# Macaron block on one core: contraction tiles of every eighth channel, both second-pass tiles of a pair transposed from blocks by way of DRAM, third layernorm's statistics on ScalarE

## The chip, the core and the metric

The kernel runs on one core of a Trainium2 chip. The metric is the device time of one execution in microseconds (us). Before the change three runs gave a median of 1308.92 us (1308.46 to 1311.21).

## What is computed

The input x has 4096 tokens of 1024 channels, all in float32. Three blocks follow each other, each on a layernorm of the running x:

```python
x = x + 0.5 * ffn(layernorm(x), weight, bias, centroids, assignments)
x = x + attn(layernorm(x), Wq, bq, Wk, bk, Wv, bv)
x = x + 0.5 * ffn(layernorm(x), weight, bias, centroids, assignments)

def ffn(x):                                  # weight 1024 x 1024, 64 centroids
    hits = softmax(x @ centroids.T / 0.1) > 0.01
    dense = x @ weight.T + bias
    return where(any(hits, 1)[:, None] & any(hits, 0)[assignments][None, :], dense, 0)

def attn(x):                                 # 32 heads of 32, 8 kv heads
    q, k, v = x @ Wq + bq, x @ Wk + bk, x @ Wv + bv
    scores = einsum('bsdh,bseh->bsde', q, repeat(k)) / sqrt(32)
    return einsum('bsde,bseh->bsdh', softmax(scores), repeat(v))
```

Attention mixes the 32 positions d of the heads within one token, not tokens. Whether a column of the FFN counts depends on all tokens (any over axis 0), so an FFN's mask is known only when every token has been seen.

## The kernel before, in words

There are NT = 32 tiles of 128 tokens. All matrix products run on TensorE, which needs the contracted channels on the partitions, so each normalised tile xn (tokens on partitions, 1024 channels in a row) has to be transposed to xT: eight groups of 128 channels, k = 0 to 7, each 128 channels by 128 tokens. Group k holds the channels 128 k to 128 k + 127, and the weights wc (FFN weight and centroids) and wqkv (the attention's three weights; the four query heads of a kv head are summed ahead) are laid out in the same groups.

There are three passes over the tokens. The first computes the first FFN before masking and writes it to DRAM (d1), the centroid gates, and the masks at its end. The second adds the masked d1 to x, does the attention, and the gate and a part of the third block's FFN. The third finishes the last FFN and stores. Most large products are in Strassen's form as Winograd wrote it: a pair of tiles is taken together, GpSimd forms four sums of their transposed halves (`token_sums`, L242 to L262), and seven smaller products take the place of eight.

The order of instructions is written out by hand: each engine's queue runs in the order in which the code issues, and DMAs are issued from the queues of SyncE (`nc.sync`), GpSimd and ScalarE, also in order. A DMA that reads what an earlier one wrote to DRAM waits on its queue until that one has landed, and what is queued behind waits too.

There are two ways to transpose. `transposed` (L198 to L207) issues eight 128x128 transposes on TensorE into two banks of PSUM, and ScalarE copies each bank out (L206); the banks are taken in turn out of four that the products use as well (`bank`, L155). In the first pass, from tile 5 on, `load_blocks` (L497) loads x in 32x32 blocks, by four DMAs whose runs are 32 channels (128 bytes), one for each strip of 32 partitions, `blocks_normed` (L511) normalises them on ScalarE and `from_blocks` (L518) transposes within the blocks on VectorE. Which block lies where makes the result a transposed tile. The statistics for them come from a second load of x.

The second pass is the loop at L1011 over stages s = 0 to 36. At stage s the tiles s to s+3 are prepared, tile b = s-2 is in the attention, g = s-3 gets its attention result added and its third layernorm, and f = s-4 and a = s-5 are transposed for the third block and gated. Stages 4 to 31 (`PAIRED`) go in pairs, even and odd. The steps of a stage that matter here, in code order:

- `load_2(s+4)`: SyncE loads x and d (d1 of that tile).
- `scores` for tile b (L1019), exponential on ScalarE (L1021).
- `project_two` (L806) gives q, k, v of the pair's tiles by seven products prod(1), (5), (6), (2), (3), (7), (4), advanced step by step by `next(two)`. Each tile's result is stored to DRAM on SyncE (qkvd, L837).
- `transposed` of xn2[s+1] (L1027), if not done yet: the second layernorm's tile.
- `keys` on GpSimd (L881), `second_added` (L967, tile g: ot times rs, then x + ot), the store of x to y2, the use of the gates.
- `sums_normed` (L183): mean and variance of tile s+2 by ScalarE, two passes over the tile with an accumulator, then a square root; its reciprocal on VectorE and the normalisation on ScalarE follow at L1069.
- `weighted` (L917): the softmax weights transposed and summed on VectorE.
- `first_added` (L473): VectorE masks d, GpSimd adds it to x, for tile s+3.
- `gate_2`, `transposed` of xn3[f] (L1074 in odd stages, L1123 in even ones), `attend` (L937) with its store to od on SyncE.
- `moments` (L158) of tile g on VectorE by BATCH_NORM_STATS, then `normed` on ScalarE: the third layernorm (L1090, L1096).
- `rearranged` (L865): SyncE loads qk (one DMA) and v (four) from qkvd; `returned`: SyncE loads ot from od.
- At the end of an odd stage the second tile of the next pair is transposed on TensorE (L1125) and GpSimd forms the pair's `token_sums` (L1126), which prod(5), prod(6), prod(3) and prod(7) of the next pair need.

Of the kernel before, what the change touches and what calls it, by code (L numbers as in the profile page):

```python
# [42 lines left out]
def kernel(  # L43
# [110 lines left out]

    def bank(name):  # L155
        return psum.tile([P, 512], F32, tag="mm", bufs=4, name=name)
# [26 lines left out]
    def sums_normed(src, name):  # L183
# [11 lines left out]
        nc.scalar.activation(xn, src, AF.Identity, bias=sc[:, 1:2], scale=sc[:, 0:1])  # L195
        yield xn

    def transposed(xn, name):  # L198

        t_ = row(f"xT_{name}").rearrange("p (k c) -> p k c", c=P)  # L200
        for h in range(2):
            tp = bank(f"tp_{name}_{h}").rearrange("p (j c) -> p j c", j=4)
            for j in range(4):
                k = 4 * h + j
                nc.tensor.transpose(tp[:, j, :], xn[:, k * P : (k + 1) * P], ident)  # L205
            nc.scalar.copy(t_[:, 4 * h : 4 * h + 4, :], tp)  # L206
        return t_  # L207
# [274 lines left out]
    with (  # L482
# [4 lines left out]
        xb = {}  # L487
# [8 lines left out]

        def load_blocks(t):  # L497

            xb[t] = row(f"xb_{t}").rearrange("p (k i c) -> p k i c", k=KT, i=4)
            src = rows(xf, t).rearrange("(i t) (k j c) -> j t k i c", i=4, j=4, k=KT)  # L500
            for j in range(4):
                nc.sync.dma_start(out=xb[t][strip(j)], in_=src[j])
# [8 lines left out]
        def blocks_normed(t, sb):  # L511
            for i in range(4):
                bi = xb[t][:, :, i]
# [3 lines left out]

        def from_blocks(t):  # L518

            b = xb.pop(t)  # L520
            t_ = row(f"xT_1_{t}")
            nc.vector.transpose(t_, b.rearrange("p k i c -> p (k i c)"))
            return t_.rearrange("p (k c) -> p k c", c=P)
# [8 lines left out]

        cn = row("cn")[:, :512]
        for h in range(2):
            nc.sync.dma_start(
                out=cn[h * NCL : (h + 1) * NCL, :], in_=cent[:, h * 512 : (h + 1) * 512]
            )
# [30 lines left out]
        def columns(c, second=nc.scalar.copy):  # L568

            for h in range(2):  # L570
                tp = bank(f"tpw{c}_{h}").rearrange("p (j c) -> p j c", j=4)
                for j in range(4):
                    k = 4 * h + j
                    nc.tensor.transpose(tp[:, j, :], wn[c][:, k * P : (k + 1) * P], ident)  # L574
# [6 lines left out]
        tp = bank("tpc").rearrange("p (j h c) -> p h j c", j=4, h=2)  # L581
        for j in range(4):
            nc.tensor.transpose(tp[:, :, j, :], cn[:, j * P : (j + 1) * P], ident)
        for h in range(2):
            nc.vector.tensor_copy(wc[:, 4 * h : 4 * h + 4, EMB:], tp[:, h])
# [6 lines left out]
        def weights(t):  # L592


            if 3 <= t < 6 or 11 <= t < 16:
# [4 lines left out]
                    out=qn, in_=wq[k * P : (k + 1) * P].rearrange("p d (g r) -> p (d g) r", r=REP)  # L600
# [8 lines left out]
            elif 16 <= t < 20:  # L609
                k = 2 * (t - 16)  # L610
                kvs = row(f"kv{k}").rearrange("p (k w c) -> p k w c", k=2, w=2)
                for i, src in ((0, wk), (1, wv)):
                    nc.sync.dma_start(
                        out=kvs[:, :, i],
# [172 lines left out]
    with (  # L787
# [223 lines left out]
        for s in range(NT + 5):  # L1011
# [4 lines left out]
            if s == NT + 1:  # L1016
                next(steps)
# [268 lines left out]
```

## Time and profile before

| | |
|---|---|
| median of 3 runs | 1308.92 us |
| the profiled execution | 1309.77 us, of which the span of its instructions is 1308.0 |
| TensorE matmul busy | 1296.1 us, 99% |
| VectorE busy | 876.9 us, 67% |
| ScalarE busy | 490.9 us, 38% |
| GpSimd busy | 602.4 us, 46% |
| granted TensorE clock | 0.997 |
| DMA | 213.44 MB, 163 GB/s; 227624 of 283475 packets under 512 B |
| a pair of stages in the second pass | 34.9 to 35.0 us |

"Busy" is the union of an engine's instructions; matmuls overlap, so a busy TensorE says only that it never ran dry. The chain is the profile's own reconstruction, back from the last instruction: at each step what released it, or what stood ahead of it on its engine. In the names of groups, `tp` is a transpose into PSUM, `qs` a product of project_two, `ff` a product of an FFN part with the centroids, `sc` and `po` the products of the attention, `ts_2q` the token sums of the second pass. PE, DVE, ACT, POOL and SPq are TensorE, VectorE, ScalarE, GpSimd and SyncE's queue. Matmuls in float32 are recorded as two instructions each, transposes as one.

### The profile page before, as it was taken

What the parts mean: (1) busy time and instruction counts of PE and PEld (TensorE: products, weight loads), DVE (VectorE), ACT (ScalarE), POOL (GpSimd) and SP (SyncE); (2) the same over time, 40 slices, a digit from 0 to 9 for tenths busy, and PEclk for the clock granted to TensorE, in tenths of its full rate; (3) what the DMA queues carried; (4) which work ended last, traced back from release to release, by engine and by line L of the source; (5) the groups of instructions that cost most, each with busy time, mean ns of one, the idle gap of its engine ahead of it and who ended that gap; (6) DMA issues with size and microseconds to landing.
All of it is one profiled execution on the core that took longest, in us unless ns stands there. A gap on an engine that the chain in (4) does not pass through costs nothing.

```text
span 1308.0 us, 22703 instructions
## 1 busy us (share of the span) xinstructions
PE 1296.1 (99%) x8734; PEld 841.4 (64%) x8734; DVE 876.9 (67%) x1798; ACT 490.9 (38%) x818; POOL 602.4 (46%) x460
## 2 busy tenths in 40 slices
PE   8999999999999999999999999999999999999998
PEld 7665777777776656666666666666666555555555
DVE  4565557555546367888888888888877448555556
ACT  4433222332211446666666666666632300000000
POOL 2622212412113247566767666666557326633440
PEclk9999999999999999999999999999999999999999
DMA  8866866776214156566666666666452347665522
GB/s 282 161 167 129 187 159 148 171 202 122 65 57 193 57 170 188 144 186 188 192 190 199 201 186 198 182 191 196 124 156 64 105 145 240 225 208 172 177 111 88
DMA packets 283475, 213.44 MB, mean 163 GB/s; under 512 B 227624, under 2 KB 242344, under 8 KB 283368
## 3 DMA queue, kind: packets, MB, share of 16 engines
q1 hardware_dynamic: 265740, 164.51, 46.2%
q0 software_dynamic: 8736, 30.68, 6.4%
q10 hardware_dynamic: 8892, 16.81, 3.6%
q8 instruction: 69, 1.13, 0.4%
q14 instruction: 38, 0.31, 0.1%
HBM read 127.77 MB, written 84.18 MB: 162 GB/s over the span
## 4 chain that ended last, share of the span: by engine, by line
PE 97%; DVE 2%; ACT 0%; DMA 0%; issue 0%; SPq 0%; ACTq 0%
PE st L286 43%; PE qs L825 20%; PE ff L212 14%; PE la L360 6%; PE tp L205 5%; PE pq L212 3%; PE sc L901 2%; PE po L943 2%; PE tpw L574 1%; DMA wn<-in_L_ffn_weight_dram 0%; PE pm L458 0%; DVE d L277 0%; DVE bn L162 0%; DVE best L426 0%; PE warm L544 0%
## 5 line engine op out<-in xcount | busy, mean ns | idle before, releaser
L251 POOL TENSOR_TENSOR ts<-xT 128x512 f32<-128x512 f32 x32 | 42.0, 1314 | 361.7 <-DVE sc L171 166.9
L277 DVE TENSOR_TENSOR d<-st,d 128x384 f32<-128x384 f32 (+1 forms) x162 | 88.8, 550 | 167.9 <-PE st L286 166.6
L212 PE MATMUL ff<-wc,xT 128*128 128x320 f32 x704 | 197.1, 433 | 1.4 <-ACT xT L206 0.6
L286 PE MATMUL st<-wc,xT 128*128 128x384 f32 x512 | 175.8, 486 | 0.0
L212 PEld LDWEIGHTS ff<-wc,xT 128*128 128x128 f32 x704 | 131.9, 190 | 56.4 <-ACT xT L206 1.9
L286 PEld LDWEIGHTS st<-wc,xT 128*128 128x128 f32 x512 | 95.9, 190 | 61.8 <-issue 0.6
L286 PE MATMUL st<-wqkv,ts 128*128 128x384 f32 (+1 forms) x392 | 131.3, 485 | 1.9 <-DVE d L277 1.9
L286 PE MATMUL st<-ws,ts 128*128 128x384 f32 x384 | 131.1, 486 | 0.0
L881 POOL TENSOR_TENSOR kd<-qk,tmask 128x1024 f32<-128x1024 f32 x32 | 60.6, 1895 | 146.2 <-DMA qk<-qkvd 146.2
L825 PE MATMUL qs<-wc,ts_2q 128*128 128x384 f32 x336 | 114.4, 490 | 0.0
L286 PEld LDWEIGHTS st<-wqkv,ts 128*128 128x128 f32 x392 | 74.7, 192 | 53.3 <-POOL x L972 2.5
L464 DVE SCALAR_TENSOR_TENSOR d<-d,qsel,mask 128x1024 f32<-128x1024 f32 (+2 forms) x68 | 106.3, 1564 | 0.2
L475 POOL TENSOR_TENSOR x<-x,d 128x1024 f32<-128x1024 f32 x32 | 75.4, 2357 | 62.7 <-DVE d L464 33.3
L277 DVE TENSOR_TENSOR d<-st,brow 128x384 f32<-128x384 f32 x96 | 52.9, 551 | 75.3 <-PE st L286 75.3
L286 PEld LDWEIGHTS st<-ws,ts 128*128 128x128 f32 x384 | 71.2, 190 | 43.0 <-issue 0.8
L165 ACT ACTIVATE mv<-mv,eps 128x1 f32<-128x1 f32 x66 | 19.4, 295 | 204.6 <-DVE mv L164 204.5
L825 PEld LDWEIGHTS qs<-wc,ts_2q 128*128 128x128 f32 x336 | 62.7, 190 | 43.6 <-issue 2.8
L206 ACT COPY xT<-tp 128x512 f32<-128x512 f32 x138 | 73.2, 582 | 44.6 <-PE tp L205 44.6
L286 PE MATMUL st<-wc,ts 128*128 128x384 f32 x256 | 87.9, 486 | 0.0
L162 DVE BATCH_NORM_STATS2 bn<-x 128x6 f32<-128x512 f32 x132 | 84.2, 680 | 3.3 <-DMA x<-in_L_attn_x_dram 3.3
L825 PE MATMUL qs<-wqkv,xT 128*128 128x384 f32 x224 | 78.3, 492 | 0.0
L972 POOL TENSOR_TENSOR x<-x,ot 128x1024 f32<-128x1024 f32 x32 | 76.3, 2384 | 2.5
(146 smaller groups left out, 2249.4 us busy)
## 6 DMA issues: line engine op xcount, KB each, us to landing
x<-in_L_attn_x_dram SPq DMA_DIRECT2D x64, 512.0 KB
d<-d SPq DMA_DIRECT2D x64, 512.0 KB
out_dram<-x ACTq DMA_DIRECT2D x30, 512.0 KB
xb<-in_L_attn_x_dram SPq DMA_DIRECT2D x108, 128.0 KB
y<-x POOLq DMA_DIRECT2D x26, 512.0 KB, 3.1
xTd<-xT POOLq DMA_DIRECT2D x26, 512.0 KB, 5.6
xT<-xTd SPq DMA_DIRECT2D x26, 512.0 KB
x<-y SPq DMA_DIRECT2D x26, 512.0 KB
```

The lines of the kernel that those rows point to most:

```text
L162: nc.vector.bn_stats(st[:, i, :], src[:, i * 512 : (i + 1) * 512])
L205: nc.tensor.transpose(tp[:, j, :], xn[:, k * P : (k + 1) * P], ident)
L206: nc.scalar.copy(t_[:, 4 * h : 4 * h + 4, :], tp)
L212: nc.tensor.matmul(p, src[:, k, :], wts[:, k, lo:hi], start=(k == 0), stop=(k == KT - 1))
L277: nc.vector.tensor_tensor(out, ps, other, ALU.add)
L286: nc.tensor.matmul(ps, src[:, k, :], wts[:, k, :], start=(k == 0 and onto is None), stop=(k == 3), skip_group_check=onto is not None,)
L360: nc.tensor.matmul(ps, src[:, k, :], wts[:, k, :], start=(k == 0 and onto is None), stop=(k == 3), skip_group_check=onto is not None,)
L464: nc.vector.scalar_tensor_tensor(d[:, sl], d[:, sl], qsel[which][:, t : t + 1], mask[:, sl], ALU.mult, ALU.mult)
L475: nc.gpsimd.tensor_tensor(xt[t], xt[t], dt_.pop(t), ALU.add)
L825: nc.tensor.matmul(ps, src[:, k, :], wts[:, k, :], start=(k == 0 and onto is None), stop=(k == 3), skip_group_check=onto is not None,)
L881: nc.gpsimd.tensor_tensor(kd, qk[:, :, D:].unsqueeze(2).to_broadcast([P, NBLK, 4, D]), tmask.unsqueeze(1).unsqueeze(3).to_broadcast([P, NB ...
L972: nc.gpsimd.tensor_tensor(xv, xv, ov, ALU.add)
```

## The change

- **Channels.** Contraction group k now holds the channels k, k + 8, k + 16 and so on. `channels` gives this view of a row, and every transpose on TensorE (FFN weight, centroids, normalised tiles) reads its data with a step of eight elements. The attention's weights are loaded in the same order from DRAM (`channel_rows`), kv by 16 DMAs instead of 8. The centroids come by one DMA to 64 partitions instead of two to 128, and are transposed by eight transposes of 64 columns instead of four of 128.
- **First pass.** `load_blocks` now loads runs of 256 channels (1 KB). `blocks_normed` works on contiguous 256 elements, and `from_blocks` reads them with a step of eight in VectorE's transpose.
- **Second pass.** For the tiles 6 to 31, none of which is transposed on TensorE for the attention any more: in an even stage s the statistics and the normalisation of tile s+2 and then of tile s+3 are computed (before, s+3 followed in the odd stage). The normalisation writes the row in another order (`by_kt`), so that a block's channels of one group are contiguous. `in_dram` stores the row to DRAM on SyncE; `load_blocks` loads it back in blocks, tile s+2 at the end of `attend` in the even stage, tile s+3 at the start of the odd stage, behind `load_2`; `from_blocks` transposes both on VectorE in the odd stage.
- **Third layernorm.** In the paired stages `sums_normed` on ScalarE takes the place of `moments` on VectorE.
- In odd stages the transposes of xn3[f] are issued ahead of prod(4) instead of behind `gate_2(a)`.

The core of the diff:

```diff
+    def channels(row):
+        return row.rearrange("p (c k) -> p k c", k=KT)
+    def channel_rows(ap):
+        return ap.rearrange("(c k) d h -> k c (d h)", k=KT)
...
-    def sums_normed(src, name):
+    def sums_normed(src, name, by_kt=False):
...
-        nc.scalar.activation(xn, src, AF.Identity, bias=sc[:, 1:2], scale=sc[:, 0:1])
+        dst = xn
+        if by_kt:
+            dst = xn.rearrange("p (j k c) -> p j c k", j=4, k=KT)
+            src = src.rearrange("p (j c k) -> p j c k", j=4, k=KT)
+        nc.scalar.activation(dst, src, AF.Identity, bias=sc[:, 1:2], scale=sc[:, 0:1])
...
-                nc.tensor.transpose(tp[:, j, :], xn[:, k * P : (k + 1) * P], ident)
+                nc.tensor.transpose(tp[:, j, :], channels(xn)[:, k], ident)
...
+    def load_blocks(t, src):
+        xb[t] = row(f"xb_{t}").rearrange("p (i c) -> p i c", i=4)
+        src = src.rearrange("(i t) (j c) -> j t i c", i=4, j=4)
+        for j in range(4):
+            nc.sync.dma_start(out=xb[t][strip(j)], in_=src[j])
+    def from_blocks(t, which, inner="c k"):
+        b = xb.pop(t).rearrange(f"p i ({inner}) -> p k i c", k=KT)
+        t_ = row(f"xT_{which}_{t}").rearrange("p (k c) -> p k c", c=P)
+        nc.vector.transpose(t_.rearrange("p k (i c) -> p k i c", i=4), b)
         return t_
...
+        def in_dram(t):
+            xnd[t] = dram.tile([P, EMB], F32, tag="xnd", bufs=4, name=f"xnd{t}")
+            nc.sync.dma_start(out=xnd[t], in_=xn2.pop(t))
...
             if has(s + 4):
                 load_2(s + 4)
+            if s + 2 in xnd:
+                load_blocks(s + 2, xnd.pop(s + 2))
...
-            if has(s + 1) and s + 1 not in xT2:
+            if paired and odd:
+                xT[f] = transposed(xn3.pop(f), f"3_{f}")
+            if s + 1 in xn2 and s + 1 not in xT2:
                 xT2[s + 1] = transposed(xn2.pop(s + 1), f"2_{s + 1}")
...
-            if has(s + 2):
-                normal = sums_normed(xt[s + 2], f"2_{s + 2}")
+            if has(s + 2) and s + 2 not in xb:
+                normal = sums_normed(xt[s + 2], f"2_{s + 2}", paired and not odd)
                 next(normal)
+            if paired and not odd:
+                third = sums_normed(xt[g], f"3_{g}")
+                next(third)
...
-            if has(s + 2):
+            if has(s + 2) and s + 2 not in xb:
                 xn2[s + 2] = next(normal)
+                if paired and not odd:
+                    in_dram(s + 2)
+                    normal = sums_normed(xt[s + 3], f"2_{s + 3}", True)
+                    next(normal)
+            if s + 1 in xb:
+                xT2[s + 1] = from_blocks(s + 1, 2, "k c")
...
                 gate_2(a)
-                xT[f] = transposed(xn3.pop(f), f"3_{f}")
             if paired and not odd:
                 fo = attend(st, qkv.pop(b)[1], b)
+                if has(s + 2):
+                    load_blocks(s + 2, xnd.pop(s + 2))
...
-            if has(g) and s != NT:
+            if paired and odd:
+                if s + 2 in xb:
+                    xT2[s + 2] = from_blocks(s + 2, 2, "k c")
+                third = sums_normed(xt[g], f"3_{g}")
+                next(third)
+            elif has(g) and not paired and s != NT:
                 mv = moments(xt[g], f"3_{g}")
...
                 between()
+                if not odd and has(s + 3):
+                    xn2[s + 3] = next(normal)
+                    in_dram(s + 3)
...
             if odd and s + 1 in PAIRED:
-                xT2[s + 2] = transposed(xn2.pop(s + 2), f"2_{s + 2}")
+                if s + 2 in xn2:
+                    xT2[s + 2] = transposed(xn2.pop(s + 2), f"2_{s + 2}")
                 ss2 = token_sums(xT2, s + 1, s + 2, "2q")
```

## The prediction

> **What bounds the kernel now.** I read the page's chain first, then the chain in order of time for one pair of stages in the middle of the second pass, then the timelines of the queues and engines there.
>
> ```profile
> PE 97%; DVE 2%; ACT 0%; DMA 0%; issue 0%; SPq 0%; ACTq 0%
> ```
>
> TensorE is the chain nearly everywhere, so a TensorE instruction taken away anywhere can be worth its full time, if what it covered is early enough. The middle pair:
>
> ```profile
> 669.40 1.00 PE sc L901 x56
> 670.40 10.52 PE qs L825 x32
> 680.92 1.00 PE po L943 x56
> 681.92 2.78 PE qs L825 x8
> 684.70 0.87 PE tp L205 x8
> 685.57 1.00 PE sc L901 x56
> 686.57 2.78 PE qs L825 x8
> 689.35 0.87 PE tp L205 x8
> 690.22 2.62 PE qs L825 x8
> 692.84 4.31 PE ff L212 x16
> 697.15 0.87 PE tp L205 x8
> 698.02 1.00 PE po L943 x56
> 699.02 1.02 PE tp L205 x8
> 700.04 4.31 PE ff L212 x16
> 704.35 1.00 PE sc L901 x56
> ```
>
> The piece after each begins where the one before ends: no wait, and the pair lasts 34.95 us (669.40 to 704.35). The transposes at 689.35 and 699.02 are those of the second layernorm, which the change takes away. Eight cost 0.87, 109 ns each. The pairs before and after are 34.9 to 35.0 too. VectorE is busy 29.4 us of each, ScalarE 23.0, GpSimd 22.7, DMA 0.62.
>
> SyncE's queue in the same pair (start, duration, what is issued):
>
> ```profile
> 686.37 0.32 SPq L837 DMA_DIRECT2D qkvd<-qkv  x1
> 688.80 0.37 SPq L869 DMA_DIRECT2D qk<-qkvd  x1
> 689.23 2.05 SPq L875 DMA_DIRECT2D v<-qkvd  x4
> 691.39 0.57 SPq L964 DMA_DIRECT2D ot<-od  x1
> 692.06 0.38 SPq L152 DMA_DIRECT2D x<-in_L_attn_x_dram  x1
> 692.49 0.42 SPq L471 DMA_DIRECT2D d<-d  x1
> 693.47 0.32 SPq L837 DMA_DIRECT2D qkvd<-qkv  x1
> 699.95 0.37 SPq L869 DMA_DIRECT2D qk<-qkvd  x1
> ```
>
> It works in order, and a load of what was just stored waits for the store: 2.43 us (686.37 to 688.80) for 384 KB on a quiet queue, 6.5 us (693.47 to 699.95) behind x and d. The latter three, 1.4 MB, take 7.9 us from the first issue.
>
> **The change, part by part.**
>
> *Transposes.* 26 tiles (6 to 31) lose 8 transposes each: 208 x 109 ns = 22.7 us of TensorE, 1.75 per pair. If nothing else became late, a pair would last 33.2 and the profiled execution 1309.77 - 22.7 = 1287.
>
> *VectorE.* Per pair it loses four BATCH_NORM_STATS2 (680 ns) and two aggregations (209): -3.1 us; it gains two 128x1024 transposes of contiguous runs (first pass: 1240): +2.5. *ScalarE* loses four copies (582) and gains, for two tiles, the two passes with their accumulator reads (1041, 194, 1148, 188): -2.3 + 5.1, so 26 of 33.2 us. Neither becomes the bound by its sum. The order matters more: in an even stage ScalarE now computes, after the exponentials, statistics of tile s+2, of g (third layernorm), normalises s+2, statistics of s+3, normalises g and s+3, all before it copies the next transposes out.
>
> *The way through DRAM.* Let E be the end of the normalisation of the odd tile s+3. Nothing in the trace shows this round trip; I build it from the rows above, in the new order of SyncE's queue.
> - The even tile was normalised 5.2 us earlier (statistics 2.4, square root 0.3, two normalisations of 1.24). Its 512 KB store takes 2.43 for 384 KB plus 0.45 for the rest: landed at E-2.3. Only then can its four block loads be issued, 0.45 each (x: 0.38, d: 0.42): E-0.5. Behind them stands the even tile's qkvd store; landed, behind 512 KB of blocks, about E+2.2.
> - The odd tile's store goes out at E+0.2, but behind it is the qk load, which waits for qkvd until E+2.2. qk, four v, ot, x and d then take what they take now, 4.1 us (688.80 to 692.91): E+6.3. Only then come the odd tile's four block loads, and they move behind x and d. x, d and blocks are 1.5 MB from E+5.3; at the 7.9 us per 1.4 MB above, E+13; part of the 7.9 was GpSimd's own stores, so I take **12.5**, with 10.2 (if qkvd is not in the way) and 13.5 as ends.
>
> What follows, up to the next E, is in-order work that I can read off (GpSimd and VectorE, same pair):
>
> ```profile
> 669.10 1.27 POOL L251 TENSOR_TENSOR ts_2q<-xT 128x512 f32<-128x512 f32 x1 [0.25 <-ACT xT L206]
> 674.13 1.90 POOL L881 TENSOR_TENSOR kd<-qk,tmask 128x1024 f32<-128x1024 f32 x1
> 676.79 2.35 POOL L972 TENSOR_TENSOR x<-x,ot 128x1024 f32<-128x1024 f32 x1
> ...
> 680.31 2.36 POOL L475 TENSOR_TENSOR x<-x,d 128x1024 f32<-128x1024 f32 x1 [0.30 <-DVE d L464]
> ```
>
> VectorE's transpose of the odd tile and, queued behind it, the masking of d for the next tile: 1.3 + 1.2 = 2.5. GpSimd's x<-x,d of that tile, which the token sums stand behind: 2.5. The four token sums, from the wait on: 5.25. kd, ot, x<-x,ot: 5.0 (674.13 to 679.14). Up to the end of x<-x,d of the following odd tile: 3.5 (to 682.67; VectorE's masking has to wait for GpSimd's x<-x,ot, 3.27 us at 676.95 where it alone takes 1.19). ScalarE then: statistics and square root 2.7 and 0.4 for the normalisation still ahead of it; normalisation of g and of the tile, 2.5. That is 24.4. With 12.5 the loop closes in **36.9 us**, more than TensorE's 33.2 and than the 34.95 of today.
>
> So the gain is not only lost: TensorE waits 3.7 us per pair, first before the second product of project_two (token sums on GpSimd), then before its prod(3), which waits for VectorE's adds behind the masking. Between 13 pairs lie 12 turns: 12 x (36.9 - 34.95) = 23; the last pair still waits at those places: about 3 more. Sum +26.
>
> *Strided reading and writing.* The 344 remaining transposes, 64 of the FFN weight and 8 of the centroids load their weights with a step of 32 bytes, and ScalarE writes 26 normalisations with a step of 128. No row has such a step. The row: a transpose's weight load takes 141 ns for 128 columns and 110 for 64 (L443), 0.48 ns per column, so some 62 ns of streaming beneath a matmul of 109. The Trainium skill ("Advanced Engine Details and Errata", SBUF Cachelines) speaks against the change: full speed needs two hits on each 16-byte line, and a new line for each element costs a penalty, which it does not size. By the row alone the cost is 0. If the rule means half speed, a load streams 124 ns: 15 ns x 416 = 6 us, much of it inside the waits just found; if the rate fell to twice the slowest row (plain loads: (190 - 103) / 96 = 0.91 ns per column, so 232 ns), 123 ns x 416 = 51 us. A gain is excluded: no load gets shorter. I take 1, being nearest to the row. For ScalarE half speed would be 0.85 x 1024 = 0.87 us per tile, twice in the loop: 12 x 1.74 = 21 us; by the row 0. I take 0.
>
> *First pass.* The blocks move in runs of 1 KB instead of 128 bytes: less DMA time, but TensorE is the chain there, so nothing. ScalarE's four normalisations per tile (586 ns) become contiguous: nothing. VectorE's transpose reads with a step; at half speed 1.07 us x 27 = 29 us, covered by VectorE's idle 11 of 29.3 us per pair; I count 0, and up to 29 if the cover failed. Eight more kv issues (0.4) lie beside that. The centroids' one DMA instead of two puts the first weight ahead by up to 0.6: -0.4; their eight transposes of 64 columns instead of four of 128: 0.
>
> Sum for the profiled execution: 1309.8 + 26 + 1 - 0.4 = 1336; the median of the runs is 0.9 lower, so 1335.5, rounded to **1336**.
>
> **Rivals.**
> - *The round trip is hidden* (the other side; 0.31). One mechanism: the odd tile's blocks land sooner than the in-order sum says. For it: DMA is idle in much of the even stage (share 0.62 per pair). Against: the stores and loads stand in one queue. It decides at a landing of 34.95 - 24.4 = 10.5 us after E: below that, faster; at 8.8 or less the pair takes TensorE's 33.2 and the time is 1286. Between these: 1286 to 1304.
> - *It cancels* (0.06): a loop of 34.8 to 35.2, 1306 to 1311.
> - *Stepped accesses cost too* (0.07): 1336 + 21 = 1357 or more.
> - *VectorE or ScalarE becomes the bound by its load*: 29 and 26 of 33.2 us speak against it; it would give about 1290 and is inside the first rival.
>
> **How the numbers follow.** Forecast (0.56): landing 11.2 to 14 gives loops of 35.6 to 38.4 and 1318 to 1356, its own range. With the first rival at 0.31 the range of 8 in 10 reaches down to 1293, leaving out a tenth, and up to 1357. A measurement tells about 0.2% (2.6 us) from no change: slower 0.63, within 0.06, faster 0.31.
>
> **What would show it.** Right: the pairs last about 37 us with TensorE idle before qs, released by GpSimd's ts_2q and by VectorE's adds; VectorE waits for the blocks' DMA before the second transpose of a pair; SyncE waits at xb for xnd and at qk for qkvd. First and third pass unchanged. Wrong: pairs of 33 to 34.5 us without idle TensorE; or transposes with more than 115 ns each; or ScalarE's normalisation near 2.1 us.

## The result and the profile after the change

The changed kernel takes 1387.58 us (median of four runs, 1384.98 to 1388.83) against 1309.09 us (1308.46 to 1311.21): a ratio of 1.0594, with a 95% interval of 1.0574 to 1.0614. The profiled span grew from 1308.0 to 1384.9 us, and the mean granted clock of TensorE fell from 0.997 to 0.969. The forecast said slower, by 27 us; it is slower by 78.

All of it lies in the second pass: its paired stages last 40 to 42 us a pair in the place of 34.9 to 35.0, thirteen times some 5.9 us. What lies ahead of stage 4 takes 1.2 us more, and what follows the start of stage 32 takes 1.8 us less.

The chain of the page, shares of the span by engine, in the changed kernel:

```profile
PE 67%; DMA 13%; POOL 6%; DVE 4%; SPq 4%; ACT 3%; issue 2%; DVEq 0%; POOLq 0%; ACTq 0%
```

TensorE carried 97% of it before. Now a third of the chain goes by way of DMA, queues and the other engines. A circle, or loop, below is a way from an instruction over others to the same instruction one pair later; no pair can be shorter than its longest circle. The chain in order of time for one pair (start, duration, what) shows one:

```profile
658.55 1.52 PE sc L908 x64
660.07 10.40 PE qs L832 x24
...
672.00 2.19 ACT xn L208
...
674.20 2.59 DMA xnd<-xn
...
678.71 5.12 DMA qkvd<-qkv
...
683.93 0.37 SPq L876
...
689.31 5.81 DMA xb<-xnd
...
696.41 1.24 DVE d L493
...
697.74 2.35 POOL x L504
...
700.18 1.52 PE sc L908 x64
```

This pair takes 41.63 us (658.55 to 700.18). In this chain TensorE is part of the circle, in its first 12 us only, and then the even tile's normalisation, its store, qkvd, SyncE's loads up to the odd tile's blocks, masking and adding follow each other. TensorE waits in one place per pair, ahead of the even stage's sc: 67.3 us in thirteen waits by the groups of instructions, where there was no wait before. The releaser named at eleven of them is GpSimd's x + d (L504), which sc does not read; at the last it is o (L962). VectorE's timeline shows what sc has to wait for (start, duration, then in brackets idle time and releaser):

```profile
695.24 1.25 DVE L235 STREAM_TRANSPOSE xT<-xb 128x1024 f32<-128x1024 f32 x1 [4.97 <-DMA xb<-xnd]
696.41 1.24 DVE L493 SCALAR_TENSOR_TENSOR d<-d,qsel,mask 128x1024 f32<-128x1024 f32 x1
...
698.40 1.52 DVE L962 SCALAR_TENSOR_TENSOR o<-po,tmask,o 128x256 f32<-128x256 f32 x3
```

sc and po share the one PSUM tile of the attention (tag "att"). The o of L962 empties it until 699.92, and sc starts at 700.18. o stands in VectorE's queue behind the odd tile's transpose, which waits 4.97 us for its blocks, and behind the reciprocal of the third layernorm (697.57), whose input ScalarE had finished at 696.32. The keys that sc reads had been there since 689.15.

The wait has a price of its own. The stretches of 655.2 to 658.5 (inside the wait), then 658.5 to 665 and 665 to 672 (columns: stretch and length, busy time of TensorE's products and weight loads, VectorE, ScalarE and GpSimd with the number of instructions, granted clock, DMA share, GB/s):

```profile
655.20:658.50 3.30, 0.00 (x0) 0.00 (x0) 3.16 (x8) 2.11 (x3) 2.40 (x2) 0.95 1.04 347
658.50:665.00 6.50, 6.45 (x72) 3.83 (x73) 2.98 (x5) 3.61 (x9) 6.42 (x5) 0.50 0.59 142
665.00:672.00 7.00, 7.00 (x23) 4.08 (x22) 5.91 (x11) 5.26 (x10) 5.90 (x5) 1.00 0.41 163
```

After the wait the clock is at half for 6.5 us, so sc and the first products of project_two take some 2.9 us longer.

### The profile page after: what moved, and what is told of

It reads as the page before. It is cut to its first block, busy times and chain, and to the rows that moved or that the text cites. A ratio compares the mean times of both kernels' runs of the same rounds, so it can differ in the third digit from the quotient of the medians.

```text
span 1384.9 us, 22461 instructions
## 1 busy us (share of the span) xinstructions
PE 1305.6 (94%) x8530; PEld 838.3 (61%) x8530; DVE 862.2 (62%) x1739; ACT 553.1 (40%) x878; POOL 601.6 (43%) x460
## 4 chain that ended last, share of the span: by engine, by line
PE 67%; DMA 13%; POOL 6%; DVE 4%; SPq 4%; ACT 3%; issue 2%; DVEq 0%; POOLq 0%; ACTq 0%
PE st L315 41%; PE qs L832 9%; PE la L389 5%; PE ff L241 5%; DMA xb<-xnd 4%; DMA qkvd<-qkv 3%; PE pq L241 3%; DMA xnd<-xn 2%; SPq L229 2%; POOL x L504 2%; ACT xn L208 2%; PE sc L908 2%; DMA qk<-qkvd 1%; POOL x L979 1%; DMA y<-x 1%
## 5 line engine op out<-in xcount | busy, mean ns | idle before, releaser
L306 DVE TENSOR_TENSOR d<-st,d 128x384 f32<-128x384 f32 (+1 forms) x162 | 88.7, 549 | 155.1 <-PE st L315 153.9
L235 DVE STREAM_TRANSPOSE xT<-xb 128x1024 f32<-128x1024 f32 x53 | 86.4, 1631 | 59.5 <-DMA xb<-xnd 59.4
L208 ACT ACTIVATE xn<-x,sc 128x1024 f32<-128x1024 f32 x58 | 95.0, 1659 | 48.0 <-DVE sc L203 47.9
L504 POOL TENSOR_TENSOR x<-x,d 128x1024 f32<-128x1024 f32 x32 | 75.3, 2352 | 86.0 <-DVE d L493 47.2
L908 PE MATMUL sc<-kd,qk 32*32 32x128 f32 x2048 | 40.0, 334 | 67.4 <-POOL x L504 58.5
L832 PE MATMUL qs<-wqkv,xT 128*128 128x384 f32 x224 | 102.8, 615 | 0.0
L306 DVE TENSOR_TENSOR d<-st,brow 128x384 f32<-128x384 f32 x96 | 52.9, 551 | 74.4 <-PE st L315 74.2
L493 DVE SCALAR_TENSOR_TENSOR d<-d,qsel,mask 128x1024 f32<-128x1024 f32 (+2 forms) x68 | 86.5, 1272 | 0.2
L196 ACT ACTIVATE xn<-x 128x1024 f32<-128x1024 f32 x58 | 61.1, 1054 | 49.4 <-POOL x L979 47.5
```

What stands on the lines that cost most here:

```text
L196: nc.scalar.activation(xn, src, AF.Identity, scale=-1.0 / EMB, accum_out=nm)
L208: nc.scalar.activation(dst, src, AF.Identity, bias=sc[:, 1:2], scale=sc[:, 0:1])
L235: nc.vector.transpose(t_.rearrange("p k (i c) -> p k i c", i=4), b)
L306: nc.vector.tensor_tensor(out, ps, other, ALU.add)
L493: nc.vector.scalar_tensor_tensor(d[:, sl], d[:, sl], qsel[which][:, t : t + 1], mask[:, sl], ALU.mult, ALU.mult)
L504: nc.gpsimd.tensor_tensor(xt[t], xt[t], dt_.pop(t), ALU.add)
```

## The experiments

Each differs from the changed kernel in the lines shown unless its text says otherwise. Where a time is that of one run, differences below 4 us are not read: that is the spread of the changed kernel's own four runs. A pair is given by the median over the paired stages.

### The parts alone

**channels_only**: the changed kernel with the loop of the second pass as before.

> Contraction groups of every eighth channel in the whole kernel and the first pass's new blocks, but the second pass's loop as before: both of its tiles are transposed on TensorE and the third layernorm's statistics are VectorE's. Theory (all of the loss comes from the second pass's new order of work, stepped weight loads cost nothing): 1309 to 1311 us, pairs of 34.9 to 35.0 us, eight transposes in 0.87 us. Rival 1 (stepped weight loads cost): 552 transposes at 15 ns more are 8 us, 1317; at twice the slowest row 1377. Rival 2 (VectorE's stepped read in the first pass is not covered): 20 us more in the first pass.

Measured: 1310.13 us (1309.36 to 1310.75), ratio 1.0008 (0.9999 to 1.0017), pairs of 35.0. Stepped weight loads and the first pass's blocks cost nothing that can be told from no change. It is not that the accesses are free. In the stepped transposes of the changed kernel and in VectorE's transpose of the first pass (minimum, median and maximum in ns):

```profile
L218 PEld LDWEIGHTS tp<-ident,xn x128: 186/190/209, 425.9 to 682.0; 128*128 128x128 f32 x128
L235 DVE STREAM_TRANSPOSE xT<-xb x15: 2020/2033/2047, 204.1 to 394.8; 128x1024 f32<-128x1024 f32 x15
```

A weight load takes 190 ns where it took 141, and VectorE 2.03 us where it took 1.24. Both are covered: eight transposes still take 0.87 us, and VectorE waits for TensorE in the first pass anyway (its adds of L306 sit idle 153.9 us for it in the changed kernel's page).

**third_only**: the kernel before, with the third layernorm's statistics by ScalarE.

```diff
+            if paired and odd:
+                third = sums_normed(xt[g], f"3_{g}")
+                next(third)
-            if has(g) and s != NT:
+            elif has(g) and not paired and s != NT:
                 mv = moments(xt[g], f"3_{g}")
...
+                if paired:
+                    xn3[g] = next(third)
```

(and the same two lines after the first statistics of even stages)

> The kernel before with only one part of the change: in the paired stages the third layernorm's statistics by ScalarE. Theory (in the kernel before o ends 0.7 us before sc needs its PSUM tile; ScalarE takes about 4 us from x + ot to the square root, VectorE with its statistics 3.1, and ScalarE's other work stands in the way): pairs of 35.4 to 36.5 us, time 1315 to 1330. Rival (it takes 3 us of VectorE's work away and is covered): 1306 to 1312.

Measured: 1310.57 us, pairs of 35.0. The rival was right: this part alone changes nothing. **third_vector** undoes it in the changed kernel:

> The changed kernel with the third layernorm's statistics back on VectorE. Theory (VectorE's queue in front of o decides): VectorE gets 3.1 us a pair more, part of it in front of o, so pairs of 40.5 to 42.5 us, time 1381 to 1405. Rival (ScalarE's new passes make the normalisations late, and the blocks with them): the first normalisation of a pair starts 2 us or more earlier after sc, pairs of 37 to 38.5 us, time 1335 to 1355.

Measured: 1397.29 us, pairs of 41.7. ScalarE's passes were not what made the changed kernel late; they save it some 10 us, which fits the theory: VectorE's queue, in which o stands, is shorter by them.

**plain_write**: `sums_normed` without `by_kt`, and `from_blocks` with "c k".

> The changed kernel, but the second pass's normalisation is written in channel order, and VectorE's transpose reads it with a step of eight elements. Theory (the step on ScalarE's write costs 0.95 us a tile, and the same step on VectorE's read 0.75): L208 all near 1.24 us, L235 all near 2.0, the loop of a pair between 40.3 and 41.0 us, time 1379 to 1388. Rival (ScalarE's stepped write is what the forecast missed): both tiles' 0.95 come off the loop, 39.1 us a pair, time 1362 or less.

Measured: 1393.43 us, pairs of 41.1, the time 5 us above the theory's range. The durations are those expected: a normalisation takes 1.24 us where the stepped write takes 2.19, and the transpose 2.00 where it takes 1.21. The step costs about as much in one place as in the other. That it may be moved without a gain does not show that it is free: with either, 0.8 to 0.95 us more a tile stands on the path from statistics to xT.

### One place at a time

**o_first**: o ahead of the odd tile's block transpose.

```diff
             if paired and odd:
+                fo = attend(st, qkv.pop(b)[1], b)
                 if s + 2 in xb:
                     xT2[s + 2] = from_blocks(s + 2, 2, "k c")
```

> The changed kernel, but in odd stages the attention's o is issued on VectorE ahead of the odd tile's block transpose (and its store ahead of the qk load on SyncE) instead of behind it; nothing is left out. Theory (TensorE waits at sc because sc writes the one PSUM tile that o has to empty, and o stands on VectorE behind the transpose that waits for the blocks' DMA): no wait before sc, a smaller one of 2 to 3 us before the second product of project_two, TensorE's clock stays up, pairs of 35 to 37 us, time 1310 to 1335. Rival (the loop through SyncE's queue and the blocks' way through DRAM has its own length of about 41 us, whoever waits for it): the wait moves to the token sums, pairs stay at 39.5 us or more, time 1368 or more.

Measured: 1381.26 us, pairs of 41.0. Half of the theory held: the wait before sc is gone. But the pair is as long, and the rival's 1368 or more is what came. Waits now stand before the products that need the token sums (12.0 us in all) and here, in the groups of TensorE between 536 and 985 us:

```profile
L218 PE MATMUL tp<-ident,xn 128*128 128x128 f32 x176 | 30.4, 311 | 37.0 <-ACT xT L219 19.7 <-ACT xn L208 17.3
```

The transposes of the third layernorm's tile wait for ScalarE, which copies out only after two normalisations. The profile's chain in one pair of the middle still runs over the blocks:

```profile
647.40 5.92 DMA xb<-xnd
...
654.61 1.24 DVE d L493
655.94 2.34 POOL x L504
658.28 1.24 POOL ts_2q L280
659.56 8.01 PE qs L832 x24
```

The circle through the blocks was not cut; only the place where TensorE waits for it has moved, from sc to the token sums.

**no_round_trip**: the blocks come from the input.

```diff
-                load_blocks(s + 2, xnd.pop(s + 2))
+                xnd.pop(s + 2), load_blocks(s + 2, rows(xf, s + 2))
```

> The changed kernel, but the blocks of the second pass are loaded from the input instead of from the stored normalised tile, so that no load waits for a store; the store stays. This leaves the first block's result and the second layernorm out of what the attention sees of these tiles. Theory (the place in the queue, not the time from store to load): SyncE no longer waits 2 us at the even tile's blocks, so qk comes 2 us sooner, but the odd tile's blocks still stand behind x and d: pairs of 38.5 to 40.5 us, time 1355 to 1381. Rival (the way out and back is what closes the loop): pairs of 36.5 us or less, 1329 or less.

Measured: 1380.12 us, pairs of 40.0, as the theory said. Waiting for the store is a small part.

**odd_on_tensor**: only the even tile by way of DRAM.

> The changed kernel, but only the even tile of a pair goes through DRAM; the odd one is transposed on TensorE at the end of the odd stage, as before. Theory (the odd tile's blocks at the end of SyncE's queue close the loop): VectorE no longer waits for blocks, 4 to 5 us off the loop, and where TensorE then doesn't run dry its clock stays up: pairs of 34.2 to 37 us, time 1300 to 1336. Rival (the even tile's way already delays qkvd and qk and with them the next pair): pairs of 38.5 us or more, 1355 or more.

Measured: 1370.52 us, pairs of 39.5: the rival. Without any odd blocks a second circle closes, by qkvd, qk, keys, x + ot, the third layernorm's statistics on ScalarE, the reciprocal, o and sc:

```profile
712.37 3.22 DMA qkvd<-qkv
...
715.64 3.16 DMA qk<-qkvd
...
718.93 1.89 POOL kd L888
...
721.59 3.33 POOL x L979
...
724.95 1.16 ACT xn L196 x2
...
728.68 0.30 ACT sd L199
...
729.01 0.17 DVE sc L202
...
731.63 1.52 PE sc L908 x64
```

**pool_queue**: the stores and block loads on GpSimd's queue.

> The changed kernel, but the stores of the normalised tiles and the block loads are issued from GpSimd's queue, which is idle for 14 us of a pair just then, instead of from SyncE's; nothing is left out. Theory (the loop is long because of the places in SyncE's in-order queue: qkvd and qk behind the even tile's blocks, the odd tile's blocks behind qk, v, ot, x and d): the odd tile's blocks land some 6 us sooner, qk is issued some 3 us sooner, pairs of 35.5 to 38 us, time 1316 to 1349. Rival (the bytes: the DMA engines are full for the last 10 us of a pair wherever the loads stand): pairs of 39.5 us or more, 1368 or more.

Measured: 1398.39 us, pairs of 41.1, in the rival's range. It is no clean test of the bytes: GpSimd then waits for the stores itself (3.3 and 4.8 us in the pair that starts at 662.5), and the keys, which it computes, start 8.3 us after qk's load is issued (683.50 to 691.81) where it is 3.3 in the changed kernel. **combined** added o_first and a masking behind the token sums:

> The changed kernel with o ahead of the odd tile's block transpose, the masking and adding of d in odd stages behind the token sums, and the way through DRAM on GpSimd's queue; nothing is left out. Theory (three waits in order on one loop): TensorE's own 33.2 us of work a pair is nearly reached, pairs of 33.5 to 36 us, time 1289 to 1322. Rival (bytes on the DMA engines): as pool_queue, 39 us or more, 1362 or more.

Measured: 1422.41 us, pairs of 43.9: the theory failed, and the time is in the rival's range, but not for the bytes as far as is seen. GpSimd's block loads there wait 8.2 us for a row buffer that TensorE's ff still reads, and with them everything behind them on GpSimd.

**sync_order**: two places in SyncE's queue.

```diff
-            if has(s + 4):
-                load_2(s + 4)
             if s + 2 in xnd:
                 load_blocks(s + 2, xnd.pop(s + 2))
+            if has(s + 4):
+                load_2(s + 4)
...
                     xn2[s + 3] = next(normal)
-                    in_dram(s + 3)
...
                 ot[b] = returned(fo, b)
+            if paired and not odd and has(s + 3):
+                in_dram(s + 3)
```

> The changed kernel with two places in SyncE's queue changed: the odd tile's store stands behind qk, v and ot instead of ahead of qk, and its block loads stand ahead of the next x and d instead of behind them; nothing is left out. Theory (the loop runs sc, prod(3), store of qkvd, load of qk, keys, x + ot, third layernorm, o, sc; the even tile's blocks and the slow clock stay in it): qkvd and qk take about 1 us less, the odd tile's blocks land about 2 us sooner, pairs of 38.5 to 40.5 us, time 1355 to 1381. Rival (the odd tile's place at the end of SyncE's queue alone closes the loop): pairs of 37.5 us or less, 1342 or less.

Measured: 1416.00 us, pairs of 43.1: slower, which neither expected. The odd tile's qkvd, stored behind the blocks, x and d, takes 8.2 us to land (700.78 to 708.95 in one pair), 1.2 us after the next sc has begun; in the changed kernel it takes 7.1 us and lands 3.2 us ahead of sc (689.84, 696.98, 700.18). That this is all of the 28 us is not shown.

**filled**: 40 transposes of the identity ahead of sc in even stages.

```diff
+            if paired and not odd and s > 4:
+                warm_2(40, f"warm{s}")
             if has(b):
                 sc = scores(qkv[b][0], kd.pop(b), b)
```

> The changed kernel with 40 more transposes of the identity (4.4 us of TensorE at full clock) ahead of sc in each even stage, where TensorE otherwise waits 4 to 6.7 us; nothing is left out. Theory (the wait lets the granted clock fall to half for 6 to 8 us, which puts prod(3), qkvd and qk 2.8 us later, and that is a part of the loop): granted clock 0.99 or more, pairs of 38 to 39 us, time 1345 to 1362, although TensorE has more to do. Rival (the low clock is only a result, and its loss would be waited for anyway): pairs of 40.5 us or more, 1380 or more.

Measured: 1380.08 us, clock 0.994, pairs of 39.3 to 41.6 (median 40.3). The clock did stay up where the filler reached to sc, and the time fell by 7.5 us, not by 37 (13 times 2.9). The rival was nearer: most of what the low clock takes would be waited for anyway.

### Places together

**early**: the even tile's normalisation straight after its statistics.

```diff
             if paired and not odd:
+                if has(s + 2):
+                    xn2[s + 2] = next(normal)
+                    in_dram(s + 2)
+                third = sums_normed(xt[g], f"3_{g}")
+                next(third)
                 if has(s + 3):
                     first_added(s + 3)
                 next(two)
...
+                if has(s + 2):
+                    load_blocks(s + 2, xnd.pop(s + 2))
                 fo = attend(st, qkv.pop(b)[1], b)
```

(with the lines taken away where they stood)

> The changed kernel with one place changed: in an even stage the even tile's normalisation is issued straight after its statistics (ahead of the third layernorm's statistics on ScalarE, of the masking of d and of prod(6)'s adds on VectorE), and its block loads ahead of the store of o. Theory (at least two loops of about 40 us run side by side, and o is still behind the odd tile's blocks and the third layernorm): pairs of 38.5 to 40.5 us, time 1355 to 1381. Rival (this place alone closes the loop, since it takes TensorE into it): pairs of 37 us or less, 1336 or less.

Measured: 1365.66 us, pairs of 39.3, as the theory said. **early_o** has o_first as well:

> The changed kernel with the even tile's normalisation early, as in the run early, and o ahead of the odd tile's block transpose, as in o_first; SyncE's queue keeps its order otherwise. Theory (these two places carry what reordered gained, SyncE's order little): pairs of 35.5 to 38 us, time 1316 to 1349. Rival (the odd tile's place at the end of SyncE's queue matters once the others are gone): pairs of 39.5 us or more, 1368 or more.

Measured: 1341.50 us, pairs of 37.1, as the theory said. The two places alone gave 21.9 and 6.3 us, together 46.1. That is what circles of about one length side by side would do: cutting one uncovers the other. **reordered** adds sync_order's two places:

> The changed kernel with all the places in the queues changed that lie on the loop: the two of sync_order; the attention's o ahead of the odd tile's block transpose on VectorE, as in o_first; and the even tile's normalisation straight after its statistics, ahead of the third layernorm's statistics on ScalarE and of the masking and prod(6)'s adds on VectorE, with its block loads ahead of the store of o, so that qkvd has nothing to wait for; nothing is left out. Theory (only the places on the loop cost, not the bytes and not the two more passes on ScalarE): no wait of TensorE over 1 us, clock 0.99 or more, pairs of 33.3 to 35 us, time 1287 to 1310. Rival (a loop elsewhere, or the bytes): pairs of 38 us or more, 1349 or more.

Measured: 1340.34 us, most pairs near 35.5 or near 40 (median 36.3). The mechanism held in part, the number did not. Against early_o SyncE's order gives nothing that can be told (1.2 us).

**tuned_sync** and **tuned** move the third layernorm's transposes back behind gate_2(a) and split the token sums:

> reordered, with the transposes of the third layernorm's tile back behind gate_2(a), where they stood before the change, so that TensorE doesn't wait for ScalarE's two normalisations, and with GpSimd's x + d of odd stages between the second and third token sum; nothing is left out. Theory (no floor but TensorE's 33.2 us): pairs of 33.3 to 35 us, time 1287 to 1310. Rival (the DMA engines' bytes, 2 MB more a pair, set a floor of about 36 to 40 us): 1322 or more.

> As tuned_sync, but with SyncE's queue in the changed kernel's order (the odd tile's store ahead of qk, its block loads behind x and d). Theory (no floor but TensorE's; SyncE's order costs up to 2 us a pair): pairs of 33.5 to 36 us, time 1290 to 1322. Rival (the odd tile's blocks behind x and d close a loop of their own): pairs of 38 us or more, 1349 or more.

Measured: 1351.70 and 1352.71 us. Both are slower than what they start from (reordered and early_o), and both lie in the rivals' ranges. What waits in tuned_sync are the products of project_two for VectorE's adds (31.4 and 16.0 us in the groups of TensorE). No version here beats the kernel before.

### No way through DRAM

**no_dram**: the same work and order on the engines, with no store, no block loads and no bytes.

```diff
-            xnd[t] = dram.tile([P, EMB], F32, tag="xnd", bufs=4, name=f"xnd{t}")
-            nc.sync.dma_start(out=xnd[t], in_=xn2.pop(t))
+            xnd[t] = xn2.pop(t)
...
-                load_blocks(s + 2, xnd.pop(s + 2))
+                xb[s + 2] = xnd.pop(s + 2).rearrange("p (i c) -> p i c", i=4)
```

> The changed kernel, but VectorE's transpose reads the normalised tile where it lies, with no store and no block loads. This leaves out the exchange of the blocks between partitions, so that the second pass's tiles are not really transposed; all work of the engines and its order stay. Theory (both close loops: without DRAM the path qk, keys, x + ot, third layernorm on ScalarE, reciprocal, o, sc is still 34.4 us or more): pairs of 34.4 to 37 us, time 1303 to 1336. Rival 1 (the forecast: the way through DRAM is the whole loss): TensorE's 33.2 us, 1287 to 1295. Rival 2 (the engines' order is nearly all of it): 38 us or more, 1349 or more.

Measured: 1314.12 us. Eight of thirteen pairs take 34.8 to 34.9 us, the others, most of them at the start, up to 36.9. The theory's range held; its path, as follows, only in part. The way through DRAM is 73.5 us of the loss. And with it gone, and with the transposes gone from TensorE, the kernel is still no faster than before. The chain of one pair in order of time:

```profile
781.62 1.06 PE sc L908 x52
782.67 10.52 PE qs L832 x32
...
797.59 2.33 DMA qkvd<-qkv
...
800.06 3.13 DMA qk<-qkvd
...
803.33 1.90 POOL kd L888
...
806.00 2.37 POOL x L979
...
816.42 1.06 PE sc L908 x52
```

and its end on ScalarE, then on VectorE:

```profile
809.47 0.37 ACT L253 COPY d<-ff 128x256 f32<-128x256 f32 x1 [4.01 <-PE ff L241]
809.74 1.06 ACT L196 ACTIVATE xn<-x 128x1024 f32<-128x1024 f32 x1
...
813.48 0.30 ACT L199 ACTIVATE sd<-sd,eps 128x1 f32<-128x1 f32 x1
...
813.80 0.16 DVE L202 RECIPROCAL sc<-sd 128x1 f32<-128x1 f32 x1 [1.07 <-ACT sd L199]
...
814.64 1.52 DVE L962 SCALAR_TENSOR_TENSOR o<-po,tmask,o 128x256 f32<-128x256 f32 x3
```

x + ot is done at 808.37. ScalarE starts the third layernorm's statistics (L196) only at 809.74, since in its queue they stand behind the copy of an ff product (L253), which waits for TensorE. The reciprocal waits for their square root; o follows to 816.16, and sc at 816.42, after a wait of 1.49 us. In seven of the eight pairs of 34.8 to 34.9 us the statistics start 28.12 us after sc, wherever x + ot is done between 26.5 and 27.8. So what closes these pairs is TensorE's unbroken work up to that ff (27.7 us), the copy, the third layernorm, o and sc (7.0 us). The way by qkvd, qk, keys and x + ot is 0.1 to 1.6 us shorter; in two of the longer pairs it is this way that closes, with x + ot done at 28.9 and 30.2 and the statistics 0.03 us later.

**no_dram_early_o**: the same for early_o.

> early_o without the way through DRAM, as in no_dram; the same exchange is left out. Theory (what early_o keeps over TensorE's 33.2 us is the DMA: 2 MB more a pair, and places in SyncE's queue): pairs of 33.2 to 34.5 us, time 1286 to 1305. Rival (ScalarE's in-order work, two more passes a tile and a slower write, holds the pair): 1322 or more.

Measured: 1330.21 us: the rival. In early_o's order the way through DRAM costs 11.3 us. What is left is that order's own. VectorE's masking of d (L493), placed so that it runs beside GpSimd's x + ot, takes 3.35 us where it takes 1.24 alone:

```profile
676.25 1.24 DVE L493 SCALAR_TENSOR_TENSOR d<-d,qsel,mask 128x1024 f32<-128x1024 f32 x1
...
687.69 3.35 DVE L493 SCALAR_TENSOR_TENSOR d<-d,qsel,mask 128x1024 f32<-128x1024 f32 x1
```

TensorE's prod(3) waits 2.0 us for the adds behind it, which makes the pairs 35.5 us; in eight of thirteen the clock then falls to half for 3.4 us, and they take 37.1.

## Why the prediction was wrong

The way by qkvd, qk and x + ot to the next sc can be measured in three kernels, from the start of sc in an even stage (us; one pair each, starting at 669.40, 781.62 and 658.55):

| | before | no_dram | changed |
|---|---|---|---|
| prod(3) done | 15.3 | 15.4 | 18.3 |
| qkvd's store issued | 17.0 | 16.0 | 20.2 |
| qk's load issued | 19.4 | 18.4 | 25.4 |
| keys start | 22.8 | 21.7 | 28.7 |
| x + ot done | 27.8 | 26.7 | 33.7 |
| third layernorm's statistics start | 29.3 | 28.1 | 33.8 |
| its reciprocal | 31.9 | 32.2 | 39.0 |
| o done | 34.3 | 34.5 | 41.4 |
| next sc | 34.95 | 34.80 | 41.63 |

Before, o is done 0.67 us before TensorE reaches the next sc. The way to it was already as long as TensorE's own work, less 2%, and nothing waited at it, so no view of waits or chains named it. Its last part hung on more than x + ot there too: VectorE's statistics of the third layernorm stand behind the gate's maximum, which waits for ScalarE's copy of an ff product:

```profile
698.25 0.23 DVE L405 TENSOR_REDUCE gmx<-ff 128x1 f32<-128x64 f32 x1 [1.57 <-ACT d L224]
...
698.71 1.28 DVE L162 BATCH_NORM_STATS2 bn<-x 128x6 f32<-128x512 f32 x2
...
701.33 0.16 DVE L171 RECIPROCAL sc<-mv 128x1 f32<-128x1 f32 x1
...
702.16 1.52 DVE L955 SCALAR_TENSOR_TENSOR o<-po,tmask,o 128x256 f32<-128x256 f32 x3
```

- *"If nothing else became late, a pair would last 33.2."* Wrong for this order of the engines. With all the new DMA gone the pair lasts 34.8, so the 1.75 us of transposes were worth 0.15. From the end of the odd stage's first ff to the next sc the copy, the third layernorm and o take 7.0 us in no_dram, and TensorE has 5.5 us of work beside them. Before, it had 7.2 (697.15 to 704.35): one group of transposes that the change takes away, and that of xn3, which it moves ahead of prod(4), stood in this stretch. This is read from two traces; no run takes the transposes alone from the kernel before. The 33.2 did not enter the time that was forecast, but the rival at 1286 and the low end of the range rest on it.
- *"The loop closes in 36.9 us"*, the loop through the blocks: **this is the step that failed**, by the size of its terms more than by its path. In the pair shown the odd tile's normalisation ends at 681.09 (E) and its blocks have landed at 695.12: 14.0 us, where 12.5 was taken and 13.5 was the upper end. But E is not on the chain, since the odd tile's blocks are issued at 687.95 without a wait for their store; the chain goes by the even tile's normalisation, which the forecast put 5.2 us ahead of E. From its end to the landing the forecast has 5.2 + 12.5 = 17.7 us, and the pair 20.9 (674.18 to 695.12). Two transfers that stand behind others were taken too short: qkvd behind the even tile's blocks, 2.7 forecast and 5.2 measured (3.1 to 5.2 in the first twelve pairs), and the odd tile's blocks behind x and d, 6.2 forecast and 7.2 measured (about 7 to 8). From the landing before (653.6) to the end of the even tile's normalisation the forecast has 24.4 - 5.2 = 19.2, and the pair 20.6. The stepped write adds 0.94 of it, a wait of ScalarE for a reciprocal adds 0.77, and the other pieces are 0.3 shorter. The reciprocal stands in VectorE's queue behind the adds that wait for TensorE's prod(6):

```profile
671.56 0.15 DVE L202 RECIPROCAL sc<-sd 128x1 f32<-128x1 f32 x1
...
672.00 2.18 ACT L208 ACTIVATE xn<-x,sc 128x1024 f32<-128x1024 f32 x1 [0.77 <-DVE sc L203]
```

This wait, by which TensorE enters the loop, is 0 to 0.77 us over the pairs. The loop of this pair closes in 41.6.
- The forecast saw one loop. The runs show a second of about 40 us (odd_on_tensor), which shares prod(3), qkvd and qk with the first, and no one place in a queue that was moved is worth more than 22 of the 78 us.
- *The stall's place* was wrong: not before project_two's second product and prod(3), but before sc, for PSUM that o had to empty. It was in the code's queue order: o behind the odd tile's transpose.
- *What DRAM adds to the second loop*, from the table up to qk's load, changed against no_dram: 2.9 us in the products (the low clock), 1.3 until qkvd is issued (behind the even tile's block loads), 2.75 until it has landed (5.22 in the place of 2.47, behind the blocks): 7.0. These are readings of one pair, and in neither pair is it this loop that closes: in no_dram the statistics stand 1.4 us behind x + ot, and in the changed kernel VectorE comes to the reciprocal 1.25 us after its input is done. no_round_trip and filled, which take the wait for the store and the low clock away one at a time, gave 7.5 us of the whole time each, as one would expect with another loop beside.
- *SyncE's order as the cause*: not borne out. With o and the normalisation moved, SyncE's two places gave nothing that can be told (reordered against early_o), and alone they cost 28 us.
- *Stepped reading*: the rule of the Trainium skill ("Advanced Engine Details and Errata", SBUF Cachelines) was right that it costs (49 ns a weight load, where the forecast's half speed would be 62), and taking nearly 0 for the time was right too, since it is covered. *The stepped write* was taken at 0; half speed, as in the forecast's other case, is what it is (2.19 against 1.24), and a normalisation near 2.1 us was one of its signs of being wrong. The rival that stepped accesses cost too (1357 or more) has the measured number in its range, but channels_only finds no cost of the reads, and in the loop above the write is 0.94 of the 4.7 us. No run has the write without the step and without the stepped read in its place, so what it costs of the 78 us is open.
- *First and third pass unchanged, VectorE's stepped transposes covered (29 us forecast, 27 times 0.79 = 21 by the rows), ScalarE not the bound by its sum*: right.

What stays open: which share of no_dram's 73.5 us is the wait, which is places in queues and which is traffic on the DMA engines. Single cuts can't be added up here.

## What to carry to other kernels

Before counting a saving on the busiest engine, look for the ways from an instruction back to itself through buffers and through the queues' order (here TensorE's ff, ScalarE's copy, the third layernorm, o and sc's PSUM tile, with qkvd, qk and x + ot close beside), and measure the slack by the end of the last releaser against the start of the engine's next use. Here it was 0.67 us of 34.95, and with 1.75 us of transposes gone the pair was 0.15 us shorter. A queue's order also decides what waits for what: an instruction that only empties a buffer should not stand behind one that waits for a long transfer. When undoing single steps gives little, undo two together before concluding that neither matters.

## What was not expected of the hardware

- TensorE's clock falls to half after short gaps, for which the forecast had no term. In the changed kernel it was 0.50 for 6.5 us after a wait of 4.35 us. In o_first two waits of 1.86 and 1.80 us with 0.7 us of transposes between them were enough (0.50 from 681.3 to 686.4), and in early_o one of three waits of 2.02 to 2.04 us (0.61 over the next 4.4 us; 1.00 after the other two). After no_dram's 1.49 us it stayed at 1.00. The Trainium skill ("TensorE: Matmul & The Clock Gate", Part 1) speaks of an idle window of about 3.4 us; these runs show it with less in one stretch. The clock records of the traces show what tells early_o's waits apart: between 500 and 1060 us the clock of a run changes only at points that lie a multiple of 3.41 us apart. Counted between such points, in seventeen runs, the full clock never fell after a stretch with up to 1.6 us of idle TensorE, fell in 21 of 57 cases after 1.6 to 2.0 us, and always after more than 2.0 (164 cases). The wait that ended at 697.59 lies whole between two points (694.36 and 697.77); those that ended at 624.08 and 660.97 are each cut in two by one (622.68 and 660.22).
- A store of 384 KB followed at once by its load took 2.4 us on a quiet queue and 5.2 us behind 512 KB of block loads in the pair shown (8.2 us behind blocks, x and d in sync_order).
- A step of 32 bytes adds 49 ns to a weight load's 141, and 0.8 us to the 1.24 of VectorE's transpose; a step of 128 bytes adds 0.95 us to the 1.24 of ScalarE's write.
